# One graph-transformer block on one core: finding each slot's token by half-precision products instead of scatters to DRAM, and broadcasting graph rows to 128 partitions

## The chip, the cores and the metric

The kernel runs on one core of a Trainium2 chip. The metric is the device time of one execution, in microseconds; the profile is of one such execution. The engines that matter are TensorE (PE in the profile, its weight loads PEld), VectorE (DVE), ScalarE (ACT), GpSimd (POOL) and SyncE (SP). SP only issues transfers and loads register values; POOL issues transfers too. The transfers of one core run on 16 DMA engines.

## The reference

The input is `x` of 1250 tokens by 768, and 20,000 graph edges `src`, `dst`. Cut to what matters:

```python
xn = _layernorm(x)
x  = x + gnn(xn, edges) + linear_attention(xn)      # gnn: two graph-attention layers (4 heads, then 2)
x  = x + ffn(_layernorm(x))

# one graph-attention layer, per head, over the edges into a token:
e = leaky_relu(s_src[src] + s_dst[dst], 0.2)
alpha = softmax of e over the edges with the same dst
out = sum of alpha * h[src]

# ffn: 8 experts, 2 chosen per token, and one shared expert
probs = softmax(x @ router_w);  gates, idx = top_k(probs, 2)
routed = sum over the two of gate * (silu(x @ w_gate[e]) * (x @ w_up[e])) @ w_down[e]
shared = silu(x @ ws_gate) * (x @ ws_up) @ ws_down
out = alpha * shared + (1 - alpha) * routed
```

## The kernel before

Tokens lie in 10 tiles of 125 (`TP = 125`, `NT = 10`), one token to a partition. All products are float32 but for the counting of edges. The stages follow each other in this order, and each engine works through its own list in order; the program's scheduler made that list once, when the kernel was built, so an instruction that waits holds back all that stand behind it on its engine. Transfers wait in the same way on the engine that issues them.

- **Counting and projection** (to about 213 us): edges are counted into a matrix of source by destination, and the first graph layer's features `G` are made.
- **Keys and values of the linear attention** (to about 396 us), with the search for each destination's largest source score beside it on DVE. `Largest` (L469) turns the scores into rows, writes them to DRAM (`rows`, L455, L466), and `head` (L478) reads one row back into a tile `ssb` in which every one of the 125 partitions holds the same 1250 numbers. `tile` (L482) takes a maximum over it.
- **Queries and output of the linear attention** (to about 583 us). Its weights `wq` come by SP (L566).
- **First graph layer** (to 735 us) and **second graph layer** (to about 910 us). `attend` (L588) loops over two halves of the destinations and the heads. For each pair it reads a row tile `r` of two rows of 625 numbers, again the same on all 125 partitions (L592, POOL), then makes for ten source tiles two exponentials (ACT, L599 and L601), a maximum and a product with the counts (DVE, L602 and L604), and multiplies the result `u` with the features on PE (L621 in the first layer, L737 in the second). `r` shares its two buffers with `ssb` (tag `ssb`). In the second layer PE gets other work between: the update products `pu` (L721), and from 899 us on the shared expert's products (L942).
- **Routing** (about 910 to 947 us): the norm of the updated tokens, written to DRAM as `xd` (L666), the router's scores, the two best experts, and for each of the 2500 pairs of token and choice a slot in the sorted order, `slot` (L893).
- **From slots to tokens**: 20 indirect scatters on POOL (L898) write each token's number to its slot in the DRAM array `who`, which had been zeroed at the start (L328). SP waits for all of them and reads `who` back as `ids`, a tile with one slot to a partition and one block of 128 slots to a column (L904). In SP's list that read stands behind the loads of the first block's weights `wg` and `wu` (L985), and ahead of 22 register loads (`value_load`, L983) and of the next weights `wd`, `wg`, `wu`. The shared expert's products (L942) run on PE meanwhile, to 992 us.
- **The expert blocks** (to about 1566 us): 22 blocks of 128 slots run always (`NSURE = 22`), up to 26 if needed (`NBLK = 26`). Block j gathers its rows by an indirect load on POOL (`gather`, L973: `xin` from `xd` by `ids`), turns them on PE (`rows`, L1008, to `ptr`), copies them on ACT (`xT`, L1009), and multiplies them with the experts' weights, of which two sets are held: `gate` (tile `pgb`), `up` (`pub`), `down` (`pdb`), all in L1002.
- **The end**: the experts' rows are gathered back (L1089), the shared expert's last product (L1097) and the sum are made, and the result is stored.

Of the kernel before, what the change touches and what calls it, by code (L numbers as in the profile page):

```python
# [19 lines left out]
P = 128  # L20
# [42 lines left out]
def gps_block(ctx: ExitStack, tc: tile.TileContext, x, src, dst, norm_g, norm_b, W1, a_src1, a_dst1, b1,  # L63
# [9 lines left out]
    who = dram.tile([NSLOT, 1], I32, name="who")  # L73
    ys = dram.tile([NSLOT, D], F32, name="ys")
    xd_t = xd.rearrange("(t p) d -> t p d", p=TP)
    who_b = who.rearrange("(b p) o -> b (p o)", p=P)
    who_p = who.rearrange("(b p) o -> p (b o)", p=P)
# [244 lines left out]
    with tc.tile_pool(name="cnt", bufs=1, reuse_waits="tile") as cp, \  # L322
            tc.tile_pool(name="tokps", bufs=2, space=PSUM, reuse_waits="tile") as ps, \
            tc.tile_pool(name="cntps", bufs=3, space=PSUM, reuse_waits="tile") as pcp:

        zero = cp.tile([P, D], F32, name="zero")
        nc.gpsimd.memset(zero, 0.0)
        nc.sync.dma_start(who_b, zero[:NBLK, :P].bitcast(I32))  # L328
# [140 lines left out]
    class Largest:  # L469
# [7 lines left out]
        def head(self, h):  # L477
            self.ssb = pmx.tile([TP, N], F32, name="ssb")  # L478
            nc.gpsimd.dma_start(self.ssb, bass.AP(tensor=self.srow.tensor, offset=self.srow.offset + h * N,
                                                ap=[[0, TP], [1, N]]))  # L480

        def tile(self, h, dt):  # L482


            junk = pmx.tile([TP, N], BF16, name="junk", bufs=1)
            nc.vector.tensor_tensor_reduce(out=junk, in0=self.ssb, in1=absent[:, dt, :], scale=1.0,  # L486
                                           scalar=-3.0e38, op0=ALU.add, op1=ALU.max,
                                           accum_out=self.mx[:, dt, h:h + 1])
# [99 lines left out]
    def attend(pw, ss, ss02, rrow, H, begin, step, finish, fill=lambda half: None):  # L588
        for half in range(2):
            for h in range(H):  # L590
                r = pmx.tile([TP, 2, W], F32, name="r", tag="ssb")
                nc.gpsimd.dma_start(r, bass.AP(tensor=rrow.tensor, offset=rrow.offset + h * N + half * W,  # L592
                                             ap=[[0, TP], [H * N, 2], [1, W]]))
                sums = begin()
                for st in range(NT):


                    ea = pw.tile([TP, W], F32, name="ea", bufs=2)
                    nc.scalar.activation(ea, r[:, 0, :], AF.Exp, bias=ss[:, st, h:h + 1])  # L599
                    eb = pw.tile([TP, W], F32, name="eb", bufs=2)  # L600
                    nc.scalar.activation(eb, r[:, 1, :], AF.Exp, bias=ss02[:, st, h:h + 1])  # L601
                    nc.vector.tensor_max(ea, ea, eb)  # L602
                    u = pw.tile([TP, W], F32, name="u", bufs=3)
                    nc.vector.scalar_tensor_tensor(u, ea, 1.0, cntT[:, st, half * W:(half + 1) * W],  # L604
                                                   op0=ALU.min, op1=ALU.mult)
                    step(sums, st, h, u)
                    fill(half)
# [204 lines left out]
    with tc.tile_pool(name="fln", bufs=2, reuse_waits="tile") as pw, tc.tile_pool(name="flnps", bufs=2, space=PSUM, reuse_waits="tile") as ps:  # L812
# [13 lines left out]
                       allow_small_or_imprecise_dtypes=True)  # L826
        rev = pw.tile([TP, NT, NE], F32, name="rev", bufs=1)
# [67 lines left out]
        puts = []  # L895
        for t in range(NT):
            for r in range(2):
                put = nc.gpsimd.indirect_dma_start(  # L898
                    out=who, out_offset=bass.IndirectOffsetOnAxis(ap=slot[:, r, t:t + 1], axis=0),
                    in_=number[:, t:t + 1], in_offset=None, bounds_check=NSLOT - 1, oob_is_err=False)  # L900
                for p in puts:
                    tc.declare_no_dep(put.ins, p.ins, reason="slots differ")
                puts.append(put)
        get = nc.sync.dma_start(ids, who_p)  # L904
        for p in puts:
            tc.add_manual_dep(get.ins, p.ins.name, mybir.DependencyInfo(
                mybir.DependencyClass.Sync, mybir.DependencyReason.DATA), reason="all slots")
# [226 lines left out]
```

## Time and profile before

| what | us |
|---|---|
| median of the 3 runs (lowest, highest) | 1626.27 (1625.15, 1630.43) |
| the profiled execution's own time | 1627.49 |
| its span, first to last instruction | 1625.8 |
| PE busy | 1528.3 (94%) |
| DVE busy | 720.8 (44%) |
| ACT busy | 368.0 (23%) |
| POOL busy | 140.4 (9%) |
| mean granted TensorE clock | 0.977 |

The profile tells, for each engine, when it was busy and what ended each idle stretch before an instruction ("idle before <- releaser"). A wait of TensorE counts in full only where nothing else of TensorE's list could run meanwhile, and since its list is fixed, that is at every wait. The granted clock is a share of full speed: at 0.5 a matmul takes about twice as long. A row of the timeline gives the start and the length of an instruction, or of several of the same kind in a row (xN); a float32 matmul shows as two records. A row of the windows gives for a stretch of time each engine's busy time, then the granted clock, the mean busy share of the 16 DMA engines, and the GB/s that they moved.

### The profile page before, as it was taken

The numbers are of one execution on the slowest core, as the hardware profiler recorded it, in microseconds if no ns is written. First come the engines' busy times: TensorE is split into PE (matmuls) and PEld (weight loads), VectorE is DVE, ScalarE is ACT, GpSimd is POOL, SyncE is SP. The second block draws the span as 40 slices with busy tenths as digits, with TensorE's granted clock in tenths as the row PEclk, the third lists the DMA queues.
The fourth block names the chain that finished last, engine by engine and source line by source line (L and its number), as shares of the span: only waits on it lengthen the run. The fifth ranks groups of instructions, "written<-read, shape, count | busy, mean of one in ns | idle before, by whom it ended". The sixth has DMA issues, their size and how long they took to land. (4 is left out here: it accounts for less than half of the span.)

```text
span 1625.8 us, 18650 instructions
## 1 busy us (share of the span) xinstructions
PE 1528.3 (94%) x7123; PEld 855.5 (53%) x7123; DVE 720.8 (44%) x1329; ACT 368.0 (23%) x630; POOL 140.4 (9%) x174
## 2 busy tenths in 40 slices
PE   6899889998999989999899998999999999999966
PEld 5566544444455678995455553444444444444433
DVE  7889639411625468996598531111111111111106
ACT  3222211111101058870367300101001111011000
POOL 2211000000000000000000142000000000000014
PEclk9999989999999999999999999999999999999988
DMA  8100042001201110002111366788888888888858
GB/s 237 39 1 1 2 128 66 4 0 38 72 20 49 30 45 32 32 17 75 32 60 48 106 92 159 293 310 315 325 315 310 306 314 314 316 319 311 308 171 262
DMA packets 104756, 238.83 MB, mean 147 GB/s; under 512 B 15735, under 2 KB 38391, under 8 KB 104663
## 3 DMA queue, kind: packets, MB, share of 16 engines
q1 hardware_dynamic: 84749, 192.43, 35.1%
q0 software_dynamic: 14544, 35.83, 7.4%
q10 hardware_dynamic: 5370, 9.30, 1.6%
q8 instruction: 63, 1.03, 0.3%
q14 instruction: 30, 0.25, 0.1%
HBM read 219.45 MB, written 18.02 MB: 146 GB/s over the span
## 5 line engine op out<-in xcount | busy, mean ns | idle before, releaser
L1002 PE MATMUL pdb<-wd,hT 128*64 128x384 f32 (+1 forms) x1056 | 176.9, 492 | 9.2 <-DMA wd<-in_L_ffn_w_down_dram 9.2
L1002 PE MATMUL pgb<-wg,xT 128*64 128x384 f32 (+1 forms) x1056 | 179.9, 491 | 0.2 <-ACT xT L1009 0.2
L1002 PE MATMUL pub<-wu,xT 128*64 128x384 f32 (+1 forms) x1056 | 174.0, 486 | 0.0
L539 PE MATMUL pp<-wkv,xnT 128*125 128x512 f32 x360 | 162.0, 599 | 0.1
L621 PE MATMUL pa<-G,u 125*125 125x199 f32 x800 | 140.4, 336 | 11.1 <-DVE h L629 6.0
L621 PEld LDWEIGHTS pa<-G,u 125*125 125x125 f32 x800 | 135.6, 189 | 16.2 <-issue 7.2
L1002 PEld LDWEIGHTS pdb<-wd,hT 128*64 128x64 f32 x1056 | 74.8, 138 | 100.7 <-issue 97.5
L1002 PEld LDWEIGHTS pub<-wu,xT 128*64 128x64 f32 x1056 | 75.6, 137 | 94.6 <-issue 94.6
L1002 PEld LDWEIGHTS pgb<-wg,xT 128*64 128x64 f32 x1056 | 74.0, 138 | 91.4 <-issue 90.6
L539 PEld LDWEIGHTS pp<-wkv,xnT 128*125 128x125 f32 x360 | 66.0, 190 | 74.0 <-issue 73.6
L1032 DVE COPY y<-pdb 128x768 f32<-128x768 f32 x22 | 21.1, 957 | 188.9 <-PE pdb L1002 188.9
L418 PE MATMUL ph<-wg,xnT 128*125 128x400 f32 x240 | 102.1, 532 | 2.7 <-PEq L432 2.6
L1021 DVE TENSOR_TENSOR h<-h,pgb 128x384 f32<-128x384 f32 x44 | 24.4, 554 | 181.0 <-ACT h L1020 181.0
L601 ACT ACTIVATE eb<-r,g_ss 125x625 f32<-125x625 f32 x120 | 95.0, 816 | 22.9 <-DVE ea L602 22.9
L602 DVE TENSOR_TENSOR ea<-ea,eb 125x625 f32<-125x625 f32 x120 | 94.0, 804 | 13.6 <-ACT eb L601 8.1
L604 DVE SCALAR_TENSOR_TENSOR u<-ea,cntT 125x625 f32<-125x625 f32 x120 | 94.0, 804 | 12.5 <-PE pa L621 8.0
L486 DVE CUSTOM_DVE_ANT_0 junk<-ssb,absent 125x1250 bf16<-125x1250 f32 x60 | 87.7, 1462 | 13.8 <-DMA ssb<-g_srow_d 12.5
L1020 ACT ACTIVATE h<-pgb 128x384 f32<-128x384 f32 x44 | 21.6, 490 | 308.2 <-PE pgb L1002 308.2
L569 PE MATMUL pq<-xnT,wq 128*128 128x500 f32 (+1 forms) x216 | 81.5, 521 | 4.5 <-DMA wq<-in_L_mix_w_qkv_dram 3.7
L721 PE MATMUL pu<-wu,xnT 128*125 128x384 f32 x240 | 82.5, 489 | 2.0 <-DVE acc L726 2.0
L1026 DVE TENSOR_TENSOR h<-h,pub 128x384 f32<-128x384 f32 x44 | 24.4, 554 | 134.4 <-PE pub L1002 134.4
L582 PE MATMUL pu<-wp,at 128*125 128x384 f32 x240 | 80.4, 488 | 1.1 <-DVE acc L585 1.1
(247 smaller groups left out, 1699.2 us busy)
## 6 DMA issues: line engine op xcount, KB each, us to landing
wg<-in_L_ffn_w_gate_dram SPq DMA_DIRECT2D x23, 2304.0 KB
wu<-in_L_ffn_w_up_dram SPq DMA_DIRECT2D x23, 2304.0 KB, 10.2
wd<-in_L_ffn_w_down_dram SPq DMA_DIRECT2D x23, 2304.0 KB
ys<-y ACTq DMA_DIRECT2D x22, 384.0 KB, 7.1
r<-g_rrow_d POOLq DMA_DIRECT2D x12, 610.4 KB, 8.3
wq<-in_L_mix_w_qkv_dram SPq DMA_DIRECT2D x18, 384.0 KB, 3.4
wkv<-in_L_mix_w_qkv_dram SPq DMA_DIRECT2D x6, 768.0 KB, 4.6
acc<-in_x_dram POOLq DMA_DIRECT2D x10, 375.0 KB, 10.8
```

Source lines behind the costliest of these rows:

```text
L418: nc.tensor.matmul(ph[:, :2 * CG], xnT[:, k, tok], wg[:, k, s * 2 * CG:(s + 1) * 2 * CG], start=(k == 0), stop=(k == KD - 1))
L486: nc.vector.tensor_tensor_reduce(out=junk, in0=self.ssb, in1=absent[:, dt, :], scale=1.0, scalar=-3.0e38, op0=ALU.add, op1=ALU.max, accum_ ...
L539: nc.tensor.matmul(pp, xnT[:, k, tok], wkv[:, k, :, :], start=(k == 0), stop=(k == KD - 1))
L569: nc.tensor.matmul(pq[:, :qw], wq[:, k, :], xnT[:, k, tok], start=(k == 0), stop=(k == KD - 1))
L582: nc.tensor.matmul(pu[:, s, :HALF], at[:, k, i * TP:(i + 1) * TP], wp[:, k, s * HALF:(s + 1) * HALF], start=(k == 0), stop=(k == KD - 1))
L601: nc.scalar.activation(eb, r[:, 1, :], AF.Exp, bias=ss02[:, st, h:h + 1])
L602: nc.vector.tensor_max(ea, ea, eb)
L604: nc.vector.scalar_tensor_tensor(u, ea, 1.0, cntT[:, st, half * W:(half + 1) * W], op0=ALU.min, op1=ALU.mult)
L621: nc.tensor.matmul(pa[i][:, :CO + 1], u[:, i * TP:(i + 1) * TP], G[:, st, h, :CO + 1], start=(st == 0), stop=(st == NT - 1))
L721: nc.tensor.matmul(pu[:, :HALF], xnT[:, k, t * TP:(t + 1) * TP], wus[s][:, k, :], start=(k == 0), stop=(k == KD - 1))
L1002: nc.tensor.matmul(pt[part, :HALF], rows[:, k, part], w[:, k, s * HALF:(s + 1) * HALF], start=(k == 0), stop=(k == KD - 1))
L1021: nc.vector.tensor_mul(h, h, pgs[s][:, :HALF])
```

## The change

Three things change.

1. The array `who`, the 20 scatters, the zero fill and the read back on SP are gone. In their place each slot is cut into its place in a block (the low 7 bits) and the block's number, both as float16. For each of the two choices DVE compares the places with 0..127 (`spot`, 125 x 10 x 128) and the block numbers with 0..25 (`numb`, 125 x 10 x 26), and multiplies `numb` by the token's number plus one. Ten matmuls per choice, with `spot` as the weights and `numb` as the moving operand, sum to a 128 x 26 table in PSUM: the token's number plus one at its slot, or zero. DVE adds the two choices' tables, subtracts one, and takes at least zero: this is `ids`. POOL makes `count16` and `number16` once, in place of `number`.
2. The row tiles `ssb` and `r` have 128 partitions instead of 125, of which 125 are read as before.
3. The 12 loads of `r` are issued by SP instead of POOL. The scheduler's list for SP then is: two `wq`, two `r`, 16 `wq`, `wu0`, six `r`, `wu1` and `wub`, three `r`, `wsg`, one `r`, `wsu`, `wsd`, and the experts' weights. The loads of `ssb` stay on POOL.

On PE the scheduler puts the first ten matmuls after the first of six `pu` matmuls of the shared expert's fourth slice, and the second ten three `pu` matmuls later. A few neighbours change places in the second graph layer's list.

```diff
-    who = dram.tile([NSLOT, 1], I32, name="who")
...
-        nc.sync.dma_start(who_b, zero[:NBLK, :P].bitcast(I32))
...
-            self.ssb = pmx.tile([TP, N], F32, name="ssb")
+            self.ssb = pmx.tile([P, N], F32, name="ssb")
             nc.gpsimd.dma_start(self.ssb, bass.AP(tensor=self.srow.tensor, offset=self.srow.offset + h * N,
-                                                ap=[[0, TP], [1, N]]))
+                                                ap=[[0, P], [1, N]]))
...
-                r = pmx.tile([TP, 2, W], F32, name="r", tag="ssb")
-                nc.gpsimd.dma_start(r, bass.AP(tensor=rrow.tensor, offset=rrow.offset + h * N + half * W,
-                                             ap=[[0, TP], [H * N, 2], [1, W]]))
+                r = pmx.tile([P, 2, W], F32, name="r", tag="ssb")
+                nc.sync.dma_start(r, bass.AP(tensor=rrow.tensor, offset=rrow.offset + h * N + half * W,
+                                             ap=[[0, P], [H * N, 2], [1, W]]))
...
+        count16 = pw.tile([TP, P], F16, name="count16", bufs=1)
+        nc.gpsimd.iota(count16, pattern=[[1, P]], base=0, channel_multiplier=0, ...)
+        number16 = pw.tile([TP, NT], F16, name="number16", bufs=1)
+        nc.gpsimd.iota(number16, pattern=[[TP, NT]], base=1, channel_multiplier=1, ...)
...
-        number = pw.tile([TP, NT], I32, name="number", bufs=1)
-        nc.gpsimd.iota(number, pattern=[[TP, NT]], base=0, channel_multiplier=1)
...
-        for t in range(NT):
-            for r in range(2):
-                put = nc.gpsimd.indirect_dma_start(
-                    out=who, out_offset=bass.IndirectOffsetOnAxis(ap=slot[:, r, t:t + 1], axis=0),
-                    in_=number[:, t:t + 1], in_offset=None, bounds_check=NSLOT - 1, oob_is_err=False)
...
-        get = nc.sync.dma_start(ids, who_p)
...
+        cut = pw.tile([TP, 2, 2, NT], I32, name="cut", bufs=1)
+        nc.vector.tensor_single_scalar(cut[:, 0], slot, P - 1, op=ALU.bitwise_and)
+        nc.vector.tensor_single_scalar(cut[:, 1], slot, P.bit_length() - 1, op=ALU.logical_shift_right)
+        cut16 = pw.tile([TP, 2, 2, NT], F16, name="cut16", bufs=1)
+        nc.vector.tensor_copy(cut16, cut)
+        pids = ps.tile([P, 512], F32, name="pids", tag="m")
+        for r in range(2):
+            spot = pw.tile([TP, NT, P], F16, name="spot", tag="xf", bufs=2)
+            nc.vector.tensor_tensor(spot, cut16[:, 0, r, :, None].to_broadcast([TP, NT, P]),
+                                    count16[:, None, :].to_broadcast([TP, NT, P]), ALU.is_equal)
+            numb = pw.tile([TP, NT, NBLK], F16, name="numb", bufs=1)
+            nc.vector.tensor_tensor(numb, cut16[:, 1, r, :, None].to_broadcast([TP, NT, NBLK]),
+                                    count16[:, None, :NBLK].to_broadcast([TP, NT, NBLK]), ALU.is_equal)
+            nc.vector.tensor_tensor(numb, numb, number16[:, :, None].to_broadcast([TP, NT, NBLK]), ALU.mult)
+            for t in range(NT):
+                nc.tensor.matmul(pids[:, r * NBLK:(r + 1) * NBLK], spot[:, t, :], numb[:, t, :], start=(t == 0),
+                                 stop=(t == NT - 1))
+        own = pw.tile([P, 2, NBLK], F32, name="own", bufs=1)
+        nc.vector.tensor_copy(own, pids[:, :2 * NBLK].rearrange("p (r b) -> p r b", r=2))
+        any_ = pw.tile([P, NBLK], F32, name="any", bufs=1)
+        nc.vector.tensor_add(any_, own[:, 0, :], own[:, 1, :])
+        nc.vector.tensor_scalar(ids, any_, -1.0, 0.0, op0=ALU.add, op1=ALU.max)
```

More of the change, by code (lines that the diff above doesn't have):

```diff
@@ L72, in gps_block @@
     xd = dram.tile([N, D], F32, name="xd")
-    who = dram.tile([NSLOT, 1], I32, name="who")
     ys = dram.tile([NSLOT, D], F32, name="ys")
     xd_t = xd.rearrange("(t p) d -> t p d", p=TP)
-    who_b = who.rearrange("(b p) o -> b (p o)", p=P)
-    who_p = who.rearrange("(b p) o -> p (b o)", p=P)
     ys_b = ys.rearrange("(b p) d -> b p d", p=P)
@@ L477, in head @@
         def head(self, h):
-            self.ssb = pmx.tile([TP, N], F32, name="ssb")
+            self.ssb = pmx.tile([P, N], F32, name="ssb")
             nc.gpsimd.dma_start(self.ssb, bass.AP(tensor=self.srow.tensor, offset=self.srow.offset + h * N,
-                                                ap=[[0, TP], [1, N]]))
+                                                ap=[[0, P], [1, N]]))
         def tile(self, h, dt):
             junk = pmx.tile([TP, N], BF16, name="junk", bufs=1)
-            nc.vector.tensor_tensor_reduce(out=junk, in0=self.ssb, in1=absent[:, dt, :], scale=1.0,
+            nc.vector.tensor_tensor_reduce(out=junk, in0=self.ssb[:TP], in1=absent[:, dt, :], scale=1.0,
                                            scalar=-3.0e38, op0=ALU.add, op1=ALU.max,
@@ L598, in attend @@
                     ea = pw.tile([TP, W], F32, name="ea", bufs=2)
-                    nc.scalar.activation(ea, r[:, 0, :], AF.Exp, bias=ss[:, st, h:h + 1])
+                    nc.scalar.activation(ea, r[:TP, 0, :], AF.Exp, bias=ss[:, st, h:h + 1])
                     eb = pw.tile([TP, W], F32, name="eb", bufs=2)
-                    nc.scalar.activation(eb, r[:, 1, :], AF.Exp, bias=ss02[:, st, h:h + 1])
+                    nc.scalar.activation(eb, r[:TP, 1, :], AF.Exp, bias=ss02[:, st, h:h + 1])
                     nc.vector.tensor_max(ea, ea, eb)
@@ L826, in gps_block @@
                        allow_small_or_imprecise_dtypes=True)
+        count16 = pw.tile([TP, P], F16, name="count16", bufs=1)
+        nc.gpsimd.iota(count16, pattern=[[1, P]], base=0, channel_multiplier=0, allow_small_or_imprecise_dtypes=True)
+        number16 = pw.tile([TP, NT], F16, name="number16", bufs=1)
+        nc.gpsimd.iota(number16, pattern=[[TP, NT]], base=1, channel_multiplier=1,
+                       allow_small_or_imprecise_dtypes=True)
         rev = pw.tile([TP, NT, NE], F32, name="rev", bufs=1)
@@ L893, in gps_block @@
         nc.vector.tensor_copy(slot, at)
-        puts = []
-        for t in range(NT):
-            for r in range(2):
-                put = nc.gpsimd.indirect_dma_start(
-                    out=who, out_offset=bass.IndirectOffsetOnAxis(ap=slot[:, r, t:t + 1], axis=0),
-                    in_=number[:, t:t + 1], in_offset=None, bounds_check=NSLOT - 1, oob_is_err=False)
-                for p in puts:
-                    tc.declare_no_dep(put.ins, p.ins, reason="slots differ")
-                puts.append(put)
@@ L904, in gps_block @@
[L904 to L907, printed above, removed]
+        cut = pw.tile([TP, 2, 2, NT], I32, name="cut", bufs=1)
+        nc.vector.tensor_single_scalar(cut[:, 0], slot, P - 1, op=ALU.bitwise_and)
+        nc.vector.tensor_single_scalar(cut[:, 1], slot, P.bit_length() - 1, op=ALU.logical_shift_right)
+        cut16 = pw.tile([TP, 2, 2, NT], F16, name="cut16", bufs=1)
```

## The prediction

> **What bounds the kernel now.** I read the page first: TensorE is busy 1528.3 of 1625.8 us, so a change gains time only where it fills one of PE's holes, and costs time where it adds to PE. So next the view of who waited for whom, for PE:
>
> ```profile
> PE pdb L1002 <- DMA wd<-in_L_ffn_w_down_dram: 9.2, 1, 9.2
> PE p_bc L208 <- DMA rb<-in_L_gnn_a_dst_dram: 7.7, 1, 7.7
> PE ptr L1008 <- DMA xin<-xd,ids: 7.7, 1, 7.7
> PE pkv L545 <- DVE vs L543: 6.1, 3, 5.6
> ...
> PE pn L737 <- DVE u L604: 6.0, 1, 6.0
> ```
>
> The change can reach three of these: the wait for the first gathered rows (7.7), the start of the second graph layer (6.0), and perhaps the `pkv` one (5.6). The timeline shows what stands behind the 6.0 (start, length, engine, line; in brackets the idle time before and its releaser):
>
> ```profile
> 784.49 11.78 PE L721 MATMUL pu<-wu,xnT 128*125 128x384 f32 x36
> 788.44 2.39 POOL L592 DMA_DIRECT2D r<-g_rrow_d  x2 [2.38 <-DMA g_rrow_d<-g_rrow]
> 798.96 0.82 ACT L599 ACTIVATE ea<-r,h 125x625 f32<-125x625 f32 x1 [13.70 <-DMA r<-g_rrow_d]
> 802.23 2.40 PE L737 MATMUL pn<-u,h 125*97 125x312 f32 x4 [5.97 <-DVE u L604]
> 804.42 1.27 PE L721 MATMUL pu<-wu,xnT 128*125 128x384 f32 x2
> 805.53 1.22 PE L737 MATMUL pn<-u,h 125*97 125x312 f32 x4
> ```
>
> "<-DVE u" names the last link only. The first `r` was issued at 788.44 and ended ACT's wait at 798.96, 10.5 us later; the first `u` needs another 3.27 us (802.23 - 798.96). PE's filler ended at 796.27. The load of `r` made this hole.
>
> Then the timeline around the first expert block:
>
> ```profile
> 983.07 1.19 POOL L898 DMA_INDIRECT who<-number,slot  x1 [0.30 <-issue]
> 986.77 5.19 PE L942 MATMUL pu<-xnT,wsu 128*128 128x500 f32 x12
> 990.33 0.37 SPq L904 DMA_DIRECT2D ids<-who  x1
> 995.54 1.07 POOL L973 DMA_INDIRECT xin<-xd,ids  x1 [11.28 <-DMA ids<-who]
> 999.64 1.51 PE L1008 MATMUL ptr<-ident,xin 128*128 128x128 f32 x6 [7.68 <-DMA xin<-xd,ids]
> ...
> 1003.43 0.37 SPq L985 DMA_DIRECT2D wd<-in_L_ffn_w_down_dram  x1
> ```
>
> The scatters ran from 947.3 to 983.1 us, the last landed near 990, the read back and the gather followed, and PE stood from 991.96 to 999.64. SP went on to the first `wd` only at 1003.43, after the read back and 22 register loads.
>
> Last, windows: busy time of PE, PEld, DVE, ACT, POOL, then granted clock, DMA share, GB/s.
>
> ```profile
> 600.90:606.00 5.10, 5.05 (x31) 4.77 (x30) 4.46 (x9) 4.14 (x6) 0.00 (x0) 1.00 0.34 123
> 249.00:251.70 2.70, 2.70 (x8) 1.01 (x6) 2.21 (x6) 0.66 (x2) 0.00 (x0) 1.00 0.91 231
> ...
> 802.00:806.00 4.00, 3.77 (x8) 2.25 (x9) 3.96 (x7) 3.88 (x6) 0.00 (x0) 0.58 0.00 0
> 999.00:1004.00 5.00, 4.36 (x18) 2.43 (x20) 0.00 (x0) 0.96 (x2) 1.00 (x1) 0.57 0.45 113
> ```
>
> The first is one `r` load alone: a third of the 16 DMA engines, 123 GB/s. The second is one `ssb` load of the same size: nearly all engines, 231 GB/s. The other two follow PE's holes: the granted clock is down to 0.58 and 0.57, so each hole costs more than its idle time.
>
> **Part 1, the row loads.** `r` is now 640 KB on 128 partitions, from SP. [...] But the `ssb` row, also one DRAM row read for all partitions, has nearly all engines and only 231 GB/s (about 250 at its peak). I take 250: 2.6 us for 640 KB, instead of 5.1. [...] If it lost some, DVE's waits on `ssb` would grow by that; a gain is bounded by the 5.6 us of `pkv`, and excluded by the engines being full already. I book 0.
>
> When does the first `r` land? The two loads are issued together, at 788.4 as before, since both wait for the same row in DRAM. Traffic aside, a `wq` load on SP spends 1.8 us (3.4 to landing, 384 KB at 236 GB/s) and an `r` on POOL 3.2 (8.3 median less 5.1); I take 2.3, nearer to SP's. The second load shares the engines: between 2.6 us (no sharing) and 5.2 (fully mixed) for the first; I take 3.6. So it lands 5.9 us after issue, at 794.3, `u` comes at 797.6, and PE waits 1.3 instead of 5.97: gain 4.7. Bounds: landing at 793 hides it all (5.97); fully mixed with 3.2, landing at 796.8, gains 2.1. With so short a hole the clock stays up: source tile 0 and its filler took 3.30 us (802.23 to 805.53), the next, at 805.53 to 807.24, took 1.71, so 1.6 more. **Sum of part 1: 6.3 us**, from 2.1 to 7.6. After that PE is nearly never idle up to 992 us, and ACT's and DVE's chains start earlier too, so it is passed on.
>
> SP's order costs nothing that I can find. The first two `r` wait for their row, landed at about 400 us; behind them `wq` number 3, which waits anyhow until PE has finished with number 1 at about 406. The six next stand behind `wu0` (583.26) and ahead of `wu1` (735.36), and were wanted from 599 to 693. Of the last four, three come before `wsg`; the fourth stands behind `wsg`, which was issued at 815.28 and waits for a `pu`, while that `r` was free to go at 838.01 only. Cover there: 22.7 us. POOL loses 12 issues of 1.2 us that nothing waited for.
>
> **Part 2, slots to tokens.** Gone are the 20 scatters, the zero fill and the read back; POOL's two fillings instead of one are at 900 us, where it stood idle until 914.67.
>
> ```profile
> L381 DVE TENSOR_TENSOR los<-lo,steps 125x1000 f16<-125x1000 f16 x20 | 23.8, 1192 | 0.0
> ...
> 81.32 0.79 PE L369 MATMUL ptc<-ident,c 125*125 125x125 f16 x10 [0.75 <-ACT c L365]
> ```
>
> `los` (group row) is the comparison of the same kind: 1192 ns for 1000 numbers, about 0.15 + 1.04 per thousand. So `spot` takes 1.48 us and each pass over `numb` 0.42. On DVE, in its built order after `slot` (946.19): two cuts, two small ones, the cast, to 947.0; `hTs_s` 0.54; `spot` 1.48; `numb` 0.42; second `spot` 1.48; the product with the numbers 0.42: about 951.2. PE reaches the first ten matmuls at 950.27 + 0.66 = 950.93, so it waits 0.3. Ten small float16 matmuls with their weights took 0.79 us (timeline row), about 0.063 each once running; the new ones are shorter, 26 columns. Twenty: 1.4 with the drain. Adding 0.2 for going in and out of the float32 sums, PE pays 1.9. From below 1.3 (no wait, 0.065 each); from above 3.2 (DVE late by 1 us, 0.11 each). The second `numb` has one buffer and waits for the first ten to finish (about 952), and is ready at 953 while PE is still at three `pu` (2.0 us): no wait. Behind it on DVE stand `own`, `ids` and the next `hTs_s`, whose PSUM is wanted only two slices on.
>
> Then `ids` is there at about 956, the first gather lands 4.0 to 8.6 us after its issue, by 965, and the shared expert covers that until 992 (27 us). PE goes straight on to `ptr`: 7.67 gained. SP's 22 register loads now run from about 949.5 to 962, so `wd` and the next `wg`, `wu` go out near 992 instead of 1003.43, and nothing in the first block is late: gate 1 wants its `wg` 19 us after the start, as before. The clock: transposes, gate and up of block 0 took 18.17 us (999.64 to 1017.81), those of a later block 16.54: 1.6 more. The first copy `xT` is now in the open: 0.2 lost. **Sum of part 2: 7.67 + 1.6 - 0.2 - 1.9 = 7.2**, from 5.5 to 8.0.
>
> The expert blocks themselves (PE 400.00 of 400 us between 1100 and 1500) and the end are untouched.
>
> **Sum.** 6.3 + 7.2 = 13.5. Against the profiled execution 1627.49 - 13.5 = 1614.0. That execution lay 1.2 above the median, so against the median 1626.27 - 13.5 = **1612.8 us**.
>
> **Rivals.** A difference of 0.3% (4.9 us) is about what a measurement of this kernel can tell from none.
>
> A. Both holes close, as above: 66%, its own range 1609.3 to 1616.5.
>
> B. The row loads land no sooner: one DRAM row read by 128 partitions could be the limit whatever the engines. [...] Part 1 then gives 1 or less: 1618. 12%.
>
> C. PE pays more for the products. DVE's list is strict, and if each `spot` took 3 us PE would wait 3.4 at the first ten and some 3 at the second, inside its own stream: part 2 gives about 1, total 1619. Against: the `los` row. 10%.
>
> D. Nothing measurable: the first block is held by something else, such as the weights `wg` and `wu`, whose issue to landing took up to 40.3 us, about to 988. They share the engines with the scatters, which go. If they still came that late, they would just fit. 1622 to 1631, 5%.
>
> E. Slower: the fourth `r` of the second layer sits behind `wsg` in SP's list. If the `pu` that frees `wsg` came after 838 instead of 815, ACT, DVE and PE would starve at the last head; every us past the load's slack (that head starts about 20 us after its load may go) counts fully, so beyond some 35 us more it outweighs part 1 and part 2. The built order puts that `pu` in the same place, hence only 7%; 1630 or more.
>
> **How the numbers follow.** Faster by over 0.3%: A, B and C, 0.88; same: D, 0.05; slower: E, 0.07. The range takes A with the bounds of both parts, and reaches to B and C: 1609.3 to 1618.9.
>
> **What would show it.** Right: no PE wait on `xin`; `ptr` within 1 us of the last `pu`; clock above 0.9 in the first 5 us of the blocks; PE's wait before the first L737 group under 3 us; an `r` load at over 0.8 DMA share; first `wd` issued within 2 us of PE's start of the blocks; twenty float16 matmuls with under 1 us of PE wait. Wrong: an ACT wait on `r` above 11 us at the second layer, a PE wait named `spot` or `numb` of several us, or a new wait on `wq`, `wg` or `wsg`.

## The result

The changed kernel takes 1607.92 us (median of four runs, 1605.36 to 1609.0); the kernel before took 1628.33 beside it (four runs, 1625.15 to 1630.43). The ratio is 0.9874, with a 95% interval from 0.985 to 0.9898: 1.3% faster, about 20 us. Forecast were 1612.8 us, 13.5 us less, and a range from 1609.3 to 1618.9. The direction and the two holes that close came as forecast; the measured time lies 1.4 us below the range.

The profiled execution of the changed kernel took 1609.0 us (span 1607.3, mean granted clock 0.985), so the two profiles differ by 18.5 us. In the view of who waited for whom, for PE:

```profile
PE pkv L541 <- DVE vs L539: 4.8, 3, 4.3
...
PE pn L733 <- DVE u L600: 0.2, 1, 0.2
```

The wait for `xin` is gone from the list, the one ahead of the second graph layer (`pn`) went from 6.0 to 0.2, and the `pkv` wait, which the forecast left as it was, from 5.6 to 4.3. The timeline of the second layer's start, after:

```profile
779.36 11.78 PE L717 MATMUL pu<-wu,xnT 128*125 128x384 f32 x36
782.77 0.91 SPq L588 DMA_DIRECT2D r<-g_rrow_d  x2
787.96 0.82 ACT L595 ACTIVATE ea<-r,h 125x625 f32<-125x625 f32 x1 [7.82 <-DMA r<-g_rrow_d]
791.23 1.29 PE L733 MATMUL pn<-u,h 125*97 125x312 f32 x4
792.36 0.81 PE L717 MATMUL pu<-wu,xnT 128*125 128x384 f32 x2
```

From the issue of the first `r` to ACT's start it is now 5.2 us (782.77 to 787.96), where it was 10.5 (788.44 to 798.96). `u` is ready before PE has finished the filler, which ends at 791.14, and PE goes straight on to `pn`. The timeline from the slots to the first block, after:

```profile
939.23 0.41 PE L911 MATMUL pids<-numb,spot 125*128 125x26 f16 x10
941.47 0.40 PE L911 MATMUL pids<-numb,spot 125*128 125x26 f16 x10
943.40 1.10 POOL L984 DMA_INDIRECT xin<-xd,ids  x1 [31.28 <-PE pu L953]
975.78 5.19 PE L953 MATMUL pu<-xnT,wsu 128*128 128x500 f32 x12
980.82 0.82 PE L1019 MATMUL ptr<-ident,xin 128*128 128x128 f32 x6
981.10 0.37 SPq L996 DMA_DIRECT2D wd<-in_L_ffn_w_down_dram  x1
981.87 7.96 PE L1013 MATMUL pgb<-wg,xT 128*64 128x384 f32 x48 [0.24 <-ACT xT L1020]
```

Neither of the two groups of products has a bracket: PE waits for neither. The first gather goes out at 943.40, with 37 us of shared expert still to come, and `ptr` follows the last `pu` without a gap. SP issues the first `wd` at 981.10, 0.3 us after that. The windows after (busy time of PE, PEld, DVE, ACT, POOL, then granted clock, DMA share, GB/s), in this order: the first pair of `ssb`, one `r` load, and the starts of the second layer and of the blocks:

```profile
222.50:224.50 2.00, 1.27 (x3) 0.20 (x2) 0.19 (x1) 0.00 (x0) 0.00 (x0) 1.00 1.02 415
595.50:597.00 1.50, 1.50 (x11) 1.50 (x10) 1.35 (x3) 1.36 (x3) 0.00 (x0) 1.00 0.98 342
791.00:795.00 4.00, 3.91 (x14) 2.15 (x14) 3.96 (x7) 3.88 (x6) 0.00 (x0) 1.00 0.00 0
981.00:986.00 5.00, 4.76 (x32) 2.32 (x32) 0.68 (x1) 0.86 (x2) 1.00 (x1) 1.00 0.78 252
```

An `r` load now has nearly all engines (0.98 instead of 0.34) and 342 GB/s instead of 123. The clock stays at 1.00 at both places where it had been 0.58 and 0.57. The first row is the surprise: `ssb` too is faster, 415 GB/s instead of 230 for such a pair before (the row is shown further down), although its DMA engines were busy all the time before.

**Where the 18.5 us lie.** A matmul of PE's list that is in both traces starts earlier after than before; the lead, from place to place, tells where the time was gained. The starts are read from the two timelines:

| up to this matmul | start before, after | lead | gained on the way | forecast |
|---|---|---|---|---|
| second group of `pc` after the first projection | 64.67, 61.27 | 3.40 | 3.40 | 0 |
| `pkv` after its long wait | 233.08, 228.11 | 4.97 | 1.57 | 0 |
| `pu` after the second layer's first `ssb` | 754.13, 748.99 | 5.14 | 0.17 | 0 |
| first `pn` of the second layer | 802.23, 791.23 | 11.00 | 5.86 | 4.7 |
| `pu` slice ahead of the products | 942.71, 931.00 | 11.71 | 0.71 | 1.6 |
| `pg` slice behind them | 954.05, 943.07 | 10.98 | -0.73 | -1.9 |
| first `ptr` of the blocks | 999.64, 980.82 | 18.82 | 7.84 | 7.67 |
| second `ptr` of block 0 | 1017.81, 997.50 | 20.31 | 1.49 | 1.4 |
| end of the span | 1625.8, 1607.3 | 18.5 | -1.81 | 0 |

The sum of the forecast's own terms that this table can test, 4.7 + 1.6 - 1.9 + 7.67 + 1.4 = 13.5, came to 5.86 + 0.71 - 0.73 + 7.84 + 1.49 = 15.2. The rest is in rows where it had nothing: 3.40 at the start, 1.74 in the two rows with `ssb`, and -1.81 at the end. The last is within what executions differ by: from the second `ptr` to the end of the span the five profiles of the kernel before took 607.2 to 609.1 us, the three of the changed kernel 609.1 to 609.8.

The start needs an explanation, since the change touches nothing of PE's there. The timeline of PE before:

```profile
60.67 4.16 PE L418 MATMUL ph<-wg,xnT 128*125 128x400 f32 x6
64.67 0.38 PE L394 MATMUL pc<-wide,los 125*125 125x500 f16 x1
```

and after:

```profile
59.26 2.18 PE L413 MATMUL ph<-wg,xnT 128*125 128x400 f32 x6
61.27 0.38 PE L389 MATMUL pc<-wide,los 125*125 125x500 f16 x1
```

These six matmuls take 4.16 us before and 2.18 after. In both they come soon after the same wait of PE for `off_i` (2.58 us, to 58.92, before; 2.53, to 58.34, after). Before, PE then ran at half clock (the granted clock was 0.5 from 57.8 to 64.7 us; in the window it is third from the end), after at full clock. Before:

```profile
59.00:62.00 3.00, 3.00 (x8) 2.06 (x9) 2.27 (x4) 0.47 (x1) 1.39 (x1) 0.50 0.02 6
```

and after:

```profile
59.00:62.00 3.00, 3.00 (x12) 1.77 (x11) 2.98 (x4) 0.39 (x1) 1.84 (x1) 1.00 0.02 5
```

Of what was issued earlier, one thing had changed: the 13 KB zero fill of `who`, issued by SP at 32.8 us, was gone.

### The profile page after: what moved, and what is told of

Same layout as the page of the kernel before. It is cut to its first block, busy times and chain, and to the rows that moved or that the text cites. A ratio compares the mean times of both kernels' runs of the same rounds, so it can differ in the third digit from the quotient of the medians.

```text
span 1607.3 us, 18656 instructions
## 1 busy us (share of the span) xinstructions
PE 1522.2 (95%) x7143; PEld 852.1 (53%) x7143; DVE 725.9 (45%) x1341; ACT 367.8 (23%) x630; POOL 104.0 (6%) x143
## 5 line engine op out<-in xcount | busy, mean ns | idle before, releaser
L600 DVE SCALAR_TENSOR_TENSOR u<-ea,cntT 125x625 f32<-125x625 f32 x120 | 93.9, 805 | 12.6 <-PE pa L617 7.8
## 6 DMA issues: line engine op xcount, KB each, us to landing
wu<-in_L_ffn_w_up_dram SPq DMA_DIRECT2D x23, 2304.0 KB, 10.2
```

## The experiments

Theory: the two closed holes are worth what the table shows; the partitions make the row loads quick, by way of the DMA engines (busy to 0.34 in an `r` load before, to 0.98 after), and they do so for `ssb` too; the start is chance. Rivals: the issuer makes the loads quick; `ssb` gains nothing (the prediction's step); the zero fill caused the half clock at the start. All are medians, each with the kernel before run beside it on the same chip. The changed kernel as it is did not run beside the four kernels that undo one step or put the fill back; the one with the fill, whose work is otherwise the same, stands in for it there.

| kernel | median us (lowest to highest, runs) | before beside it | ratio, 95% interval |
|---|---|---|---|
| slots to tokens alone | 1617.4 (1616.79 to 1618.69, 5) | 1630.01 (19 runs) | 0.9926, 0.9914 to 0.9939 |
| row loads alone | 1622.8 (1620.31 to 1624.64, 5) | 1630.01 | 0.9959, 0.9946 to 0.9971 |
| `ssb` on 128 alone | 1628.9 (1624.24 to 1633.06, 14) | 1630.01 | 0.999, 0.9978 to 1.0003 |
| the change again | 1608.82 (1606.66 to 1609.71, 4) | 1630.01 | 0.9872, 0.9857 to 0.9886 |
| the change, `ssb` on 125 | 1611.64 (1611.15 to 1613.6, 4) | 1632.27 (9 runs) | 0.9877, 0.986 to 0.9894 |
| the change, `r` by POOL | 1611.28 (1609.46 to 1612.49, 4) | 1632.27 | 0.9874, 0.9858 to 0.989 |
| the change, `r` on 125 | 1611.42 (1610.93 to 1612.69, 4) | 1632.27 | 0.9875, 0.9859 to 0.9891 |
| the change with the zero fill | 1607.67 (1605.05 to 1617.58, 6) | 1632.27 | 0.9846, 0.983 to 0.9862 |
| the change, a third time | 1609.04 (1605.62 to 1610.53, 5) | 1632.79 (9 runs) | 0.9862, 0.9837 to 0.9887 |
| row writes by ScalarE | 1608.57 (1608.38 to 1608.8, 4) | 1632.79 | 0.9862, 0.9835 to 0.989 |
| row writes by ScalarE, `ssb` by SyncE | 1602.35 (1600.83 to 1605.29, 5) | 1632.79 | 0.9826, 0.9802 to 0.9851 |

### Each part alone

Slots to tokens alone: the change without its hunks for `ssb` and `r`, which stay as before.

```diff
-        nc.sync.dma_start(who_b, zero[:NBLK, :P].bitcast(I32))
...
-                put = nc.gpsimd.indirect_dma_start(
...
-        get = nc.sync.dma_start(ids, who_p)
...
+                nc.tensor.matmul(pids[:, r * NBLK:(r + 1) * NBLK], spot[:, t, :], numb[:, t, :], start=(t == 0),
```

> The second part alone: each slot's token comes from the float16 products, and the scatters, the zero fill and the read back are gone; the r and ssb loads stay as before (125 partitions, both issued by POOL). Theory (each hole is worth what the two traces show at its place): the wait for the first gathered rows closes (7.8 us), the clock dip after it goes (1.5), the products cost 0.7, so 8.6 us under the kernel before; PE's hole ahead of the second graph layer stays near 6 us and the pkv wait near 5.6. Rival 1 (the gain at the very start, 3.4 us before 65 us in the profile of the changed kernel, is caused by the missing zero fill): about 12 us under the kernel before, and the half clock at 57 to 65 us absent in this profile. Rival 2 (the parts help each other: without the early second layer the first gather is late again): under 7 us.

Row loads alone: only those hunks.

```diff
-            self.ssb = pmx.tile([TP, N], F32, name="ssb")
+            self.ssb = pmx.tile([P, N], F32, name="ssb")
...
-                nc.gpsimd.dma_start(r, bass.AP(tensor=rrow.tensor, offset=rrow.offset + h * N + half * W,
-                                             ap=[[0, TP], [H * N, 2], [1, W]]))
+                nc.sync.dma_start(r, bass.AP(tensor=rrow.tensor, offset=rrow.offset + h * N + half * W,
+                                             ap=[[0, P], [H * N, 2], [1, W]]))
```

> The first part alone: r to 128 partitions and issued by SyncE, ssb to 128 partitions issued by POOL; the scatters, the zero fill and the read back stay. Theory: the hole ahead of the second graph layer closes (5.9 us), the clock dip after it goes (1.3), the two stretches that wait for ssb gain 1.3 and 0.6, and some 0.7 is given back in the second layer, so about 8 us under the kernel before; the wait for the first gathered rows stays at about 7.7. Rival (the missing zero fill causes the gain at the very start): the same 8 us, with the half clock at 57 to 65 us there as in the kernel before. The two parts done alone add up to the whole difference less what belongs to the start: about 17 of 20 us if the start is chance or belongs to neither.

And the whole change beside them, as it is:

> The changed kernel itself once more, on the same chip as its parts, as a yardstick for them: about 18 to 20 us under the kernel before. If the gain at the start is chance (the phase at which the clock is granted), its profile may or may not show the half clock at 57 to 65 us, and the time is then up to 3.4 us longer; if the missing zero fill causes it, the half clock is absent there again.

Measured: 12.6 us for the slots, 7.2 for the rows, 21.2 for both together: the parts add up to 19.8, so by these medians they neither help nor hinder each other much. Each closes its own hole and leaves the other. Timeline of PE with the slots alone:

```profile
800.55 2.40 PE L733 MATMUL pn<-u,h 125*97 125x312 f32 x4 [5.78 <-DVE u L600]
...
991.82 0.82 PE L1019 MATMUL ptr<-ident,xin 128*128 128x128 f32 x6
```

and who waited for whom with the rows alone:

```profile
PE ptr L1008 <- DMA xin<-xd,ids: 7.5, 1, 7.5
...
PE pkv L545 <- DVE vs L543: 5.0, 2, 4.5
```

The rows' 7.2 us fit the expected 8. The slots' 12.6 do not fit the expected 8.6, and in this profile the half clock at 57 to 65 us was absent: by this run alone, the rival with the zero fill was ahead. So the fill was tried by itself.

### The zero fill put back

```diff
+    who = dram.tile([NSLOT, 1], I32, name="who")
+    who_b = who.rearrange("(b p) o -> b (p o)", p=P)
...
+        nc.sync.dma_start(who_b, zero[:NBLK, :P].bitcast(I32))
```

> The changed kernel with the 13 KB zero fill put back at its old place in SyncE's list; nothing reads what it fills. It is for the 3.4 us that the profile of the changed kernel gained before 65 us. Theory (the clock is granted in windows of 3.4 us that run freely, and where they fall on the 2.6 us wait near 56 to 59 us is chance from one execution to the next): the same time as the changed kernel within 1 us. Rival (the fill delays something there, and so causes the half clock at 57 to 65 us): 1.7 to 3.4 us more, about 1611, and the half clock there in its profile.

Measured: 1607.67, against 1607.92, 1608.82 and 1609.04 for the changed kernel in the other comparisons. The fill costs nothing that can be told. Its profile was of an odd execution, the one at 1617.58. Two windows of it, with the granted clock third from the end:

```profile
47.00:56.00 9.00, 8.86 (x27) 7.57 (x25) 7.13 (x27) 1.75 (x2) 0.97 (x2) 0.50 0.00 0
56.00:66.00 10.00, 10.00 (x19) 5.47 (x19) 3.74 (x11) 0.80 (x1) 1.23 (x1) 0.50 0.06 17
```

Here a wait of 2.2 us (of PE for ACT, at 40.6 us) was followed by half clock until 66 us, and this execution lost 6.8 us at the start against the first profile of the kernel before. The rival falls by the medians, and a later profile of the kernel before, with the fill in it, had full clock throughout this stretch (below).

The clock records of the traces say more. In each of the 17 profiles the starts and ends of half clock lie on one grid of 3.413 us, to within 0.01 us. Where this grid lies against the first instruction differs from execution to execution, also of the same kernel. Four of the five profiles of the kernel before have half clock here, and three of these have a twin without the fill, at nearly the same place of the grid:

| profile | zero fill | place of the grid us | half clock between 40 and 66 us |
|---|---|---|---|
| before, first | yes | 3.22 | 57.8 to 64.7 |
| row writes by ScalarE, `ssb` by SyncE | no | 3.18 | 57.8 to 64.6 |
| before, second | yes | 0.94 | 52.1 to 59.0 |
| the change, a third time | no | 0.85 | 52.1 to 58.9 |
| before, fourth | yes | 1.98 | 60.0 to 63.4 |
| row writes by ScalarE | no | 1.90 | 59.9 to 63.3 |
| the change, first | no | 1.99 | none |

So none of these three stretches needs the fill. The place of the grid doesn't decide alone: at 1.98 and 1.99 one profile has half clock and one has none. Half clock between 40 and 66 us was in seven of the eight profiles with the fill and in four of the nine without, too few to exclude that the fill makes it more frequent; the medians show no cost of that.

### What the kernel before really loses

Four more profiles of the kernel before, unchanged.

> The kernel before once more, for a second profile of it: the slot part alone was 12.6 us faster by the medians, and 8 us by the holes that it closes. Theory (where the free-running clock windows fall on the small waits is chance, and the first profile of the kernel before was a good execution): the holes keep their places and lengths (pkv 5.6, the second layer 6.0, the first gathered rows 7.7, each within 0.5 us), and the time differs from the first profile by several us through the granted clock alone, the most at the start, before 70 us. Rival (the scatters land at very different times from one execution to the next): the wait for the first gathered rows differs by more than 2 us from 7.7.

> The kernel before, a third profile. Theory (the wait for the first gathered rows in the kernel before is not a fixed 7.7 us: the scatters and their read back land at different times, 7.5 to 9.2 us of wait in the four profiles so far that have them; together with the clock windows at the start this spreads its time over 8 us, and the first profile lay at the low end): a wait of 7.5 us or more, longer where the time is longer. Rival (only the granted clock varies): a wait within 1 us of 7.7 whatever the time.

> The kernel before, a fourth profile; as for the third: a wait for the first gathered rows of 7.5 us or more, longer where the time is longer, or, by the rival, within 1 us of 7.7 whatever the time.

> The kernel before, a fifth profile; as for the third: a wait for the first gathered rows of 7.5 us or more, longer where the time is longer, or, by the rival, within 1 us of 7.7 whatever the time.

PE's wait for the first gathered rows, in the second profile of the kernel before and in the fifth:

```profile
PE ptr L1008 <- DMA xin<-xd,ids: 9.2, 1, 9.2
```

```profile
PE ptr L1008 <- DMA xin<-xd,ids: 5.0, 1, 5.0
```

| profile of the kernel before | time us | wait for `xin` | wait of `pn` | wait of `pkv` | lead on the first profile at 66 us |
|---|---|---|---|---|---|
| fifth | 1620.0 | 5.0 | 5.6 | 5.8 | 3.7 |
| third | 1621.19 | 5.3 | 5.4 | 5.9 | 1.9 |
| first | 1627.49 | 7.7 | 6.0 | 5.6 | 0 |
| second | 1628.05 | 9.2 | 5.7 | 5.9 | 1.4 |
| fourth | 1628.48 | 9.1 | 5.6 | 5.6 | 1.3 |

The waits of `pn` and `pkv` hold within 0.6 us; the wait for the first gathered rows does not, 5.0 to 9.2. For the second profile I had expected all three waits within 0.5 us of the first; at 9.2 us this one was not. My floor of 7.5 us for the later ones was wrong too, but the long waits went with the long times, as expected, and "within 1 us of 7.7 whatever the time" fell. Time at the start varies by another 3.7 us, with the fill always there. The fifth profile had the full clock there:

```profile
59.00:62.00 3.00, 3.00 (x11) 1.68 (x10) 2.76 (x4) 0.12 (x1) 1.84 (x1) 1.00 0.02 5
```

So the start differs from execution to execution whatever the kernel, and the slots' part takes away a wait whose length differs too: 7.7 us is the value of one execution. In place, from the first `pn` to the second `ptr` of block 0, the five profiles of the kernel before took 213.0 to 218.5 us (median 215.6), the one with the slots alone 208.0: 7.6 us less, near the expected 8.6. That the other 5 of the 12.6 us are longer waits and the start is likely, but not shown: the medians of the kernel before beside the experiments, 1630 to 1633, lie above all five of its profiles.

### One line alone, and undone: `ssb`

```diff
-            self.ssb = pmx.tile([TP, N], F32, name="ssb")
+            self.ssb = pmx.tile([P, N], F32, name="ssb")
-                                                ap=[[0, TP], [1, N]]))
+                                                ap=[[0, P], [1, N]]))
```

> One line of the change alone: the ssb rows go to 128 partitions instead of 125, still issued by POOL; all else as before. Theory (the 16 DMA engines carry a 128-partition broadcast faster even where all of them were busy with the 125-partition one): ssb lands in a median of about 4.9 us instead of 6.2, its packets move at some 400 GB/s instead of 231 to 250, the first pkv wait goes from 5.6 to 4.3, and the kernel is 1.5 to 2 us faster. The prediction's own step (it gains nothing, since the engines were full already): landing 6.2, no change in time. Rival (ssb landed sooner in the changed kernel only because r left POOL's queue): landing 6.2, no change either.

> The changed kernel with one step undone: ssb back to 125 partitions (still by POOL). Theory: ssb lands in a median of about 6.2 us again, the pkv wait goes from 4.3 back to 5.6 and the second layer's wait from 1.2 to 1.8, so 1.5 to 2 us above the changed kernel (about 1610.5). The prediction's own step (nothing): about 1608.5, the same as the changed kernel, and a landing of 4.9.

Alone on the kernel before it gave 1.1 us, with an interval that reaches across zero: that kernel varies too much to tell. Undone in the changed kernel it costs 4.0 us against the run with the zero fill beside it on the same chip (1611.64 - 1607.67), and but for that one odd execution their ranges don't meet. The size is less sure: against the changed kernel's medians on other chips it is 2.6 to 3.7 us, and the ratios to the kernel before (0.9877 against 0.9862 to 0.9874) make it 0.5 to 2.4. In place, from 200 to 760 us, it gains 2.5 us less than the changed kernel (its lead on the first profile goes from 2.93 to 2.46, where the changed kernel's goes from 3.06 to 5.14), but 1.7 of that comes from 3.4 us more of half clock near 400 us. Over all profiles the same way (last `ptc` of the counting to `pu` after the second layer's first `ssb`) took a median of 558.8 us (556.8 to 559.8) in the seven with `ssb` on 125 partitions and 556.9 (555.5 to 557.9) in the eight with 128 by POOL and the row writes as before: 1.9 us. The windows with the first pair of loads, before:

```profile
226.00:228.00 2.00, 1.43 (x4) 0.36 (x2) 0.00 (x0) 0.00 (x0) 0.00 (x0) 1.00 1.03 230
```

with the one line alone:

```profile
224.00:226.00 2.00, 1.23 (x3) 0.19 (x1) 0.39 (x1) 0.00 (x0) 0.00 (x0) 1.00 1.03 423
```

and with it undone in the changed kernel:

```profile
223.00:226.00 3.00, 0.80 (x2) 0.00 (x0) 0.00 (x0) 0.00 (x0) 0.00 (x0) 1.00 0.99 229
```

The DMA share is 1 in all three, and the rate 230, 423, 229 GB/s. The `pkv` wait was 4.2 us with the one line alone and 6.0 with it undone. It was 5.6 to 6.0 us in all seven profiles with 125 partitions and 4.2 to 4.5 in all those with 128 by POOL. The prediction's step falls, and so does the rival that `ssb` gained only because `r` left POOL's queue: in the run with the one line alone, `r` was still there.

### Partitions against issuer: `r`

```diff
-                nc.sync.dma_start(r, bass.AP(...
+                nc.gpsimd.dma_start(r, bass.AP(...
```

> The changed kernel with r issued by POOL again, still on 128 partitions: partitions against issuer. Theory (the partitions make it, because all 16 DMA engines carry the load): r lands within 5 us of its issue, the hole ahead of the second graph layer stays under 1.5 us, and the time is within 1.5 us of the changed kernel. Rival (the issuer makes it): r lands in about 8 us, the hole is 5 to 6 us again, and the time is about 7 us above the changed kernel.

```diff
-                r = pmx.tile([P, 2, W], F32, name="r", tag="ssb")
+                r = pmx.tile([TP, 2, W], F32, name="r", tag="ssb")
-                                             ap=[[0, P], [H * N, 2], [1, W]]))
+                                             ap=[[0, TP], [H * N, 2], [1, W]]))
```

> The changed kernel with r on 125 partitions again, still issued by SyncE: the other half of that question. Theory: an r load alone takes about 5 us of transfer at a third of the DMA engines (some 125 GB/s), lands about 7 us after its issue, the later of a pair 10 us, the hole ahead of the second layer is 4.5 to 6 us, and with the clock dip the time is 6 to 7 us above the changed kernel. Rival (the issuer makes it): a landing within 5 us, no hole, no difference.

The start of the second layer with `r` by POOL on 128 partitions:

```profile
783.00 1.44 POOL L588 DMA_DIRECT2D r<-g_rrow_d  x2 [2.25 <-DMA g_rrow_d<-g_rrow]
788.71 0.82 ACT L595 ACTIVATE ea<-r,h 125x625 f32<-125x625 f32 x1 [8.77 <-DMA r<-g_rrow_d]
791.97 1.29 PE L733 MATMUL pn<-u,h 125*97 125x312 f32 x4 [1.03 <-DVE u L600]
```

and by SyncE on 125:

```profile
784.72 0.77 SPq L588 DMA_DIRECT2D r<-g_rrow_d  x2
792.76 0.82 ACT L595 ACTIVATE ea<-r,h 125x625 f32<-125x625 f32 x1 [10.69 <-DMA r<-g_rrow_d]
796.03 2.32 PE L733 MATMUL pn<-u,h 125*97 125x312 f32 x4 [2.96 <-DVE u L600]
```

| `r` | issue to ACT's start us | PE's wait at `pn` us |
|---|---|---|
| 125, POOL (before) | 10.5 | 6.0 |
| 125, SyncE | 8.0 | 3.0 |
| 128, POOL | 5.7 | 1.0 |
| 128, SyncE (the change; two later profiles) | 5.2; 5.6, 5.7 | 0; 0.6, 0.6 |

The partitions do more: 5.0 us of the wait by POOL, 2.4 to 3.0 by SyncE. But the issuer does half of it where the partitions are 125, which my theory gave nothing; there POOL took 10.0 to 10.5 us in seven profiles and SyncE 8.0 in one. With 128 partitions the issuer makes no difference that these profiles show. It is not bandwidth: a window of one 125-partition load by SyncE,

```profile
598.00:602.00 4.00, 4.00 (x26) 4.00 (x25) 3.36 (x6) 3.65 (x5) 0.00 (x0) 1.00 0.32 126
```

has the third of the engines and the 126 GB/s that it had by POOL (0.34, 123). A window of one 128-partition load by POOL has 0.98 of the engines:

```profile
597.00:598.00 1.00, 1.00 (x8) 1.00 (x7) 0.85 (x2) 1.00 (x2) 0.00 (x0) 1.00 0.98 400
```

By the medians each of the two kernels costs 3.6 to 3.8 us against the run with the fill on the same chip. For the 125 partitions that is little more than the 3.0 us of the hole, and less than the expected 6 to 7. For POOL it is more than the 1.0 us of its hole and than the 1.5 that I expected at most; its one profile, of its lowest time, doesn't show the rest, and its ratio to the kernel before, 0.9874, is no worse than the changed kernel's (0.9862 to 0.9874), so that a cost beyond the hole is not shown.

### Beyond the change: the rest of the round trip

That the issuer counted for `r` on 125 partitions pointed at what POOL still issues: the write of the two rows of scores to DRAM, and the `ssb` loads behind it.

```diff
-        nc.gpsimd.dma_start(d, r[:n, :])
+        nc.scalar.dma_start(d, r[:n, :])
```

> Beyond the change: the two row writes of each layer (the row that ssb reads back, and the one that r reads back) are issued by ScalarE, which has just made the row, instead of POOL; the loads stay as in the changed kernel. In the profile of the changed kernel the first such write took 5.4 us from issue to the moment when POOL could go on, and ssb landed 6.6 us after that, while DVE and then PE stood. Theory (the issuer matters for the latency: r on 125 partitions left a hole of 3.0 us when issued by SyncE and 6.0 by POOL): each write lands 2 to 3 us sooner, the pkv wait of 4.3 us shrinks to about 2, and the time falls by 2 to 4 us. Rival (the write's time is DRAM's, not the queue's): nothing.

```diff
-            nc.gpsimd.dma_start(self.ssb, bass.AP(...
+            nc.sync.dma_start(self.ssb, bass.AP(...
```

> The same with the ssb loads issued by SyncE as well, so that nothing in the round trip through DRAM is issued by POOL. Theory: another 1 to 2 us off the wait for the first ssb, the pkv wait near zero, and 3 to 6 us under the changed kernel in all, which would beat both kernels. Rival (the ssb loads stand in SyncE's list ahead of a pair of weight loads and wait there for their row, so that these come late): a new wait of pp for its weights near 240 to 260 us, and no gain or a loss.

With the changed kernel as the yardstick on the same chip:

> The changed kernel again, as the yardstick on the same chip for the two that follow: 18 to 22 us under the kernel before, about 1608.

The writes alone gave nothing (1608.57 against 1609.04), as the rival had it: the write took 4.6 us from issue to the next step instead of 5.4, and the load behind it, by POOL, 7.8 instead of 6.7. With both moved it is 1602.35, 6.7 us under the changed kernel beside it, and the two ranges don't meet. The loads moved without the writes were not run, so the loads' share alone is open. The first round trip through DRAM in the changed kernel:

```profile
212.21 0.53 POOL L461 DMA_DIRECT2D g_srow_d<-g_srow  x1 [2.09 <-ACT g_srow L459]
217.65 1.10 POOL L475 DMA_DIRECT2D ssb<-g_srow_d  x2 [4.91 <-DMA g_srow_d<-g_srow]
...
224.31 1.46 DVE L482 CUSTOM_DVE_ANT_0 junk<-ssb,absent 125x1250 bf16<-125x1250 f32 x1 [7.23 <-DMA ssb<-g_srow_d]
```

and with both moved:

```profile
215.53 0.50 ACTq L461 DMA_DIRECT2D g_srow_d<-g_srow  x1
...
220.32 0.81 SPq L475 DMA_DIRECT2D ssb<-g_srow_d  x2
...
225.12 1.46 DVE L482 CUSTOM_DVE_ANT_0 junk<-ssb,absent 125x1250 bf16<-125x1250 f32 x1 [4.45 <-DMA ssb<-g_srow_d]
...
228.91 0.68 PE L541 MATMUL pkv<-vs,ks 125*128 125x129 f32 x4 [1.55 <-DVE vs L539]
```

From the write's issue to DVE's first maximum it is 9.6 us, against 12.1 in the changed kernel (12.0 to 12.2 in its three profiles); the load's part is 4.8, against 6.7. The longest `pkv` wait fell from 4.3 to 1.6, and the longest of the second layer's `pu` for its first `ssb` from 1.2 to 0.2, 3.7 us together. Clock is much of the rest: in the changed kernel half clock followed the `pkv` wait (227.3 to 234.1 us in the first profile, 3.4 us of it in the other two), here none did. The weights behind `ssb` in SyncE's list were not late: PE has no wait for `wkv`. This version has the lowest median of all that ran.

## Why the prediction was wrong

**Right.** No PE wait on `xin`; `ptr` directly behind the last `pu`; clock 1.00 at the start of the blocks; the wait at the first `pn` under 3 us; an `r` load at 0.98 of the engines; the first `wd` 0.3 us after the blocks' start; no PE wait at the products. Of the cases, A came true in its mechanism.

**Right in size too.** Closing the `xin` hole and the clock behind it: 9.07 forecast, 9.33 found against that one profile. The cost of DVE from the `los` row: `spot` 1.48 and `numb` 0.42 us, as worked out.

**The step that failed, on `ssb`: "a gain ... excluded by the engines being full already. I book 0."** Busy engines are not engines at their rate. `ssb` on 125 partitions had the 16 engines busy at 230 GB/s, on 128 it has them busy at 415 to 423. That is worth 1.7 us in the table and 1.9 over all profiles; the medians of the run with it undone would give more, up to 4.0. For `r` on 128 partitions I took 250 GB/s from this same `ssb` row, an estimate; measured were 342 to 400. The `ssb` row was no limit of such loads; it was a slow load.

**Mis-sized.** The first `r` was forecast 5.9 us after its issue and came after 5.2, but the transfer in that sum was too slow: 2.6 us at 250 GB/s, where 640 KB at the measured 342 to 400 GB/s take 1.6 to 1.9. So the hole closed whole, 5.86 instead of 4.7. The products: -1.9 forecast, -0.73 found. Ten of them took 0.41 us, not 0.7, and DVE was in time. No run shows the 0.2 us that the sum had for going in and out of the float32 sums; the 0.73 is what both groups cost with all that belongs to them. The clock behind the `r` hole: 1.6 forecast; 1.3 us came with the first two source tiles (from a lead of 11.00 to 807.24 - 794.91 = 12.33) and 0.6 went again by the end of the layer, 0.7 in all. That the clock stays up behind a hole of about 1 us held in the profile that has one: behind the 1.0 us wait with `r` by POOL on 128 partitions the first `pn` row (x4) took 1.29 us, as in the changed kernel, where it took 2.32 behind the 3.0 us wait with `r` by SyncE on 125. The issuer: the forecast gave it 0.9 us (2.3 beside the transfer, where POOL's loads had 3.2). At 125 partitions it made no difference to the bandwidth (126 GB/s by SyncE, 123 by POOL), but ACT could start 2.0 to 2.5 us sooner with SyncE's load. At 128, which the change uses, 5.2 to 5.7 us against 5.7 show no such difference.

**What the sum left out.** It was made against one execution, "1626.27 - 13.5", as if that execution's waits were the kernel's. The kernel before spreads from 1620 to 1636 us over the runs here; its five profiles, from 1620 to 1628, differ in a wait of 5.0 to 9.2 us and in the clock at the start. The changed kernel stays within 1605 to 1611. The range had nothing for this. The bounds of its two parts add up to 7.6 + 8.0 = 15.6 us at most, or 1610.7 us; its lower end, 1609.3, is not what they give. The same terms came to 15.2, within these bounds.

With the sizes found and the same start, the profiled execution would have taken 1627.49 - 15.2 - 1.7 + 1.8 = 1612.4, where its forecast was 1614.0; the other 3.4 us, down to 1609.0, were the start's. More profiles agree on what the change does in place: from the last `ptc` of the counting to the second `ptr` of block 0 the five profiles of the kernel before took 817.6 to 825.2 us (median 822.5), the three of the changed kernel 805.4 to 806.0 (805.6). That is 16.9 us where 13.5 were forecast; half of the difference is the terms that were mis-sized (15.2 - 13.5), half is `ssb`. The rest of the 20 to 24 us between the medians of the runs is not placed: most executions of the kernel before beside the experiments took longer than any that was profiled.

## What to carry to other kernels

A broadcast row load can be worth widening by a few partitions, here from 125 to 128 (an `r` load went from 123 GB/s to between 342 and 400, a pair of `ssb` loads from 230 to between 415 and 423), also where the profile shows all DMA engines busy: compare its GB/s with the best load of the trace before calling it full. For a short load on the critical path the time from issue to use counts, not the transfer alone, and the issuer can be part of it (on 125 partitions 10.0 to 10.5 us by POOL, 8.0 by SyncE). And where a wait stands at the end of a chain of many small transfers, as the 5.0 to 9.2 us behind the twenty scatters, take its length from several profiles before it goes into a sum.

## What was not expected of the hardware

- **The `ssb` load of 125 rows moved at about half the rate of the one of 128, with the 16 engines equally busy** (230 GB/s against 415 to 423, at a share of 1.02 to 1.03). In the first pair of `ssb` loads one 5000-byte packet took a median of 364 ns in the first profile of before and 345 ns with that line undone, with 128 partitions 194 ns. `r` on 125 partitions kept a third of the engines busy and its packets were not slow: 123 to 126 GB/s at a share of 0.32 to 0.34, with a median of 199 ns for a 5000-byte packet in the first profile of before. Why the packets of the 125-row load by POOL are slow was not tried.
- **The same wait is followed by no half clock, by 3.4 us or by 6.8 us of it.** The stretches of half clock before 260 us lasted 3.4, 6.8 or 10.2 us in all profiles, apart from the odd one. Behind the same 2.6 us wait at 56 to 59 us, 6.8 us of it began at 57.8 in the first profile of before, 3.4 us at 59.4 with the rows alone, and none in the changed kernel. The boundaries lie on a grid of 3.413 us, and its place against the first instruction differed between executions of one kernel, from 0.35 to 3.22 us in the five of before. At 66 us the executions of all kernels lay between 6.8 us behind and 3.7 us ahead of the first profile, with work on PE that was the same.
- **A chain of twenty small scatters and their read back has no fixed end**: as a wait of PE, it was 5.0 to 9.2 us in five executions of one program.
